# A graph attention kernel: layer 0's output transposed by the DMA crossbar, part of the D splits on GpSimd, two plain float32 v products in the prologue, and a new order of work

## Chip, cores, metric

One core of a Trainium2 chip. The metric is device time in microseconds, the median of some runs of the whole kernel; lower is better. In the profiles PE is TensorE, DVE is VectorE, ACT is ScalarE and POOL is GpSimd; SBUF is the memory on the chip that holds the tiles, and PSUM the one that TensorE writes its products to.

## The reference, cut to what matters

128 batch items x of 128 tokens by 512 features, a 128x128 adjacency `adj`. Layer 0 is a product with `adj`, a row maximum, a residual and a layer norm; layer 1 is attention with 8 heads under the mask `adj`, a projection, a layer norm and a residual, and one more norm.

```python
def L0(x, W1, W2, b):            # W1 = W2 = adj
    A = einsum('od,bdn->bon', W1, x);  C = einsum('od,bdn->bon', W2, x) + b[None, :, None]
    return max(relu(A[:, :, None, :] + (C - A)[:, :, :, None]), axis=-1)
def L1(x, w_qkv, w_proj, b_proj, gamma, beta, mask):
    q, k, v = split(x @ w_qkv)   # 8 heads
    a = softmax(where(mask == 0, -inf, q @ k.T * scale))
    o = (a @ v) @ w_proj + b_proj
    return o + layernorm(o) * gamma + beta
x = layernorm(x + L0(x, adj, adj, b))
x = layernorm(x + L1(x, w_qkv, w_proj, b_proj, gamma, beta, adj))
```

## The kernel before: the parts concerned

The kernel works in 32 groups of four items. Dense products are float32 made of float32r ones: each operand is split into a high part (a mask), a low part (a subtraction) and D, a combination of the two. HALF is 4096. Step (g, j) is a dense product of group g: 0 to 3 are v, 4 to 11 are q and k. "po" is the projection. `pm` and `pd` are the two PSUM tiles of one product, main and D; `pp` holds both in a double bank.

```python
def split(key, src, dsts):                       # VectorE: mask and low part
    _, fl, _ = dsts
    xh = work.tile([P, KC, P], FP, tag="xh")
    nc.vector.tensor_scalar(xh.bitcast(I32), src.bitcast(I32), HIGH, None, op0=ALU.bitwise_and)
    hs[key] = dsts, xh
    nc.vector.tensor_tensor(fl, src, xh, op=ALU.subtract)
def split_d(key):                                # VectorE, from its own mask xh
    (_, fl, fd), xh = hs[key]
    nc.vector.scalar_tensor_tensor(fd, fl.bitcast(FP), -HALF, xh, op0=ALU.mult, op1=ALU.add)
def split_high(key):                             # ScalarE
    (fh, _, _), xh = hs[key]
    nc.scalar.copy(fh, xh)
def transpose_x(b):                              # TensorE, into PSUM
    pts[b] = ps_1.tile([P, KC, P], FP, tag="ps1")
    for c in range(KC):
        nc.tensor.transpose(pts[b][:, c, :], xs[b][:, c * P : (c + 1) * P], ident)
def relu_0(b, n):                                # GpSimd, a few columns; then ScalarE adds it to x
    nc.gpsimd.tensor_scalar(r, r, b0_sb, 0.0, op0=ALU.add, op1=ALU.max)
def residual_x(b):                               # GpSimd, 128x512, all in SBUF
    nc.gpsimd.tensor_scalar(xbs[b], xbs[b], *c0s.pop(b), op0=ALU.mult, op1=ALU.add)
    nc.gpsimd.tensor_tensor(xbs[b], xbs[b], beta_sb, op=ALU.add)
# ... dense_main evicts pm (ScalarE), dense_rest adds pd (VectorE), conv, scores, softmax, norms cut
O = {...}     # positions of every part, in us of a planned TensorE time
plan.sort()   # the sorted plan fixes each engine's order; every engine runs its queue in that order
```

## Time and profile before

| what | value |
|---|---|
| time | 1993.17 us (1991.69 to 1994.87) |
| start of dense work, period of a steady group | 24.81 us, 60.47 us (32 groups) |
| one group of TensorE, DVE, ACT, POOL | 59.6, 51.3, 48.2, 30.7 us busy |

TensorE sets the period. The other engines have 9 us or more of slack a group on average; the kernel gives each of them one queue in a fixed order. The lines are in the prediction.

### The profile page before, as it was taken

What the parts mean: (1) busy time and instruction counts of PE and PEld (TensorE: products, weight loads), DVE (VectorE), ACT (ScalarE), POOL (GpSimd) and SP (SyncE); (2) the same over time, 40 slices, a digit from 0 to 9 for tenths busy, and PEclk for the clock granted to TensorE, in tenths of its full rate; (3) what the DMA queues carried; (4) which work ended last, traced back from release to release, by engine and by line L of the source; (5) the groups of instructions that cost most, each with busy time, mean ns of one, the idle gap of its engine ahead of it and who ended that gap; (6) DMA issues with size and microseconds to landing.
All of it is one profiled execution on the core that took longest, in us unless ns stands there. A gap on an engine that the chain in (4) does not pass through costs nothing. (4 is left out here: it accounts for less than half of the span.)

```text
span 1990.6 us, 33310 instructions
## 1 busy us (share of the span) xinstructions
PE 1921.3 (97%) x11041; PEld 1483.2 (75%) x11041; DVE 1676.0 (84%) x2615; ACT 1557.1 (78%) x4130; POOL 984.9 (49%) x1744
## 2 busy tenths in 40 slices
PE   6999999999999999999999999999999999999995
PEld 4777777777777777777777777777777777777774
DVE  7798888888888988888988888888889888888887
ACT  5887877778887778877778877788777788777875
POOL 2164455554555544554545555545555445545456
PEclk8999999999999999999999999999999999999998
DMA  4334444444443444454444444444434444444341
GB/s 121 108 107 128 127 117 126 119 127 128 116 128 106 117 133 127 112 135 120 117 128 121 123 123 117 130 129 113 132 106 117 133 128 112 136 119 117 107 112 58
DMA packets 337340, 237.90 MB, mean 120 GB/s; under 512 B 266512, under 2 KB 270736, under 8 KB 337168
## 3 DMA queue, kind: packets, MB, share of 16 engines
q1 hardware_dynamic: 336880, 235.72, 42.8%
q8 instruction: 87, 1.43, 0.3%
q14 instruction: 85, 0.70, 0.1%
q10 hardware_dynamic: 288, 0.07, 0.0%
HBM read 72.16 MB, written 98.57 MB: 86 GB/s over the span
## 5 line engine op out<-in xcount | busy, mean ns | idle before, releaser
L339 ACT ACTIVATE e<-e,nmax 128x128 f32<-128x128 f32 x1024 | 395.8, 389 | 21.6 <-DVE nmax L332 21.6
L437 ACT ACTIVATE square<-o,sum 128x512 bf16<-128x512 f32 x256 | 184.4, 720 | 145.2 <-DVE o L431 144.0
L354 ACT COPY planes<-e 128x2048 uint16<-128x2048 uint16 x124 | 234.3, 1889 | 60.8 <-DVE e L348 55.3
L443 POOL TENSOR_SCALAR sum<-sum 128x1 f32<-128x1 f32 (+1 forms) x322 | 82.5, 256 | 375.2 <-ACT square L437 369.2
L426 POOL TENSOR_TENSOR xb<-xb,o 128x512 f32<-128x512 f32 x124 | 203.9, 1645 | 85.3 <-DVE o L431 85.3
L444 POOL TENSOR_TENSOR sum<-sum,mhalf 128x1 f32<-128x1 f32 (+1 forms) x322 | 224.8, 698 | 26.8
L449 POOL TENSOR_SCALAR sum<-sum 128x1 f32<-128x1 f32 x256 | 82.4, 322 | 272.5 <-DVE o L431 271.2
L339 ACT ACTIVATION_READ_ACCUMULATOR e<-e,nmax 128x1 f32 x1024 | 192.6, 188 | 0.0
L409 POOL TENSOR_TENSOR xb<-xb,beta_sb 128x512 f32<-128x512 f32 x128 | 165.3, 1292 | 10.7
L348 DVE TENSOR_TENSOR e<-e,sums 128x1024 f32<-128x1024 f32 x128 | 166.8, 1303 | 4.4
L324 DVE SCALAR_TENSOR_TENSOR e<-psc,mask 128x1024 f32<-128x1024 f32 x128 | 153.3, 1218 | 18.4 <-PE psc L312 18.4
L464 ACT ACTIVATE o<-o,sum 128x512 f32<-128x512 f32 x128 | 103.7, 810 | 71.9 <-POOL sum L452 71.9
L332 DVE TENSOR_REDUCE nmax<-e 128x8 f32<-128x1024 f32 x128 | 155.0, 1211 | 0.0
L312 PEld LDWEIGHTS psc<-qkT 64*128 64x128 f32 x2048 | 124.3, 187 | 34.6 <-issue 23.5
L312 PE MATMUL psc<-qkT 64*128 64x128 f32 x2048 | 148.4, 285 | 0.0
L385 PE MATMUL pav<-eT,v 128*64 128x128 f32 x2048 | 133.0, 277 | 0.3 <-ACT eT L376 0.2
L179 PE MATMUL pa<-xt,adjT 128*128 128x512 f32 x256 | 126.9, 600 | 0.6 <-DVE adjT L104 0.4
L408 POOL TENSOR_SCALAR xb<-xb,sum 128x512 f32<-128x512 f32 x128 | 110.8, 866 | 23.4 <-DMA xb<-in_x_dram 22.9
L385 PEld LDWEIGHTS pav<-eT,v 128*64 128x64 f32 x2048 | 109.8, 137 | 13.7 <-issue 5.2
L456 DVE SCALAR_TENSOR_TENSOR o<-o,sum,gamma_sb 128x512 f32<-128x512 f32 x128 | 108.0, 844 | 1.0 <-POOL sum L449 0.8
L431 DVE SCALAR_TENSOR_TENSOR o<-o,sum,xb 128x512 f32<-128x512 f32 x128 | 99.0, 773 | 11.0 <-POOL sum L444 1.4
L225 PE MATMUL ptx<-ident,xt 128*128 128x128 f32 x512 | 85.2, 290 | 23.5 <-ACT xt L218 11.3
(4782 smaller groups left out, 5536.8 us busy)
## 6 DMA issues: line engine op xcount, KB each, us to landing
rows<-planes SPq DMA_DIRECT2D x124, 512.0 KB, 3.0
xt<-in_x_dram SPq DMA_DIRECT2D x128, 256.0 KB, 3.1
xb<-in_x_dram SPq DMA_DIRECT2D x128, 256.0 KB, 2.9
out_dram<-o SPq DMA_DIRECT2D x128, 256.0 KB, 2.1
wraw<-in_L_gnn_w_qkv_dram SPq DMA_DIRECT2D x12, 256.0 KB, 3.0
eT<-rows SPq DMA_TRANSPOSE x124, 4.9
wraw<-in_L_gnn_w_proj_dram SPq DMA_DIRECT2D x4, 256.0 KB, 4.4
gamma_sb<-in_L_gnn_ln_gamma_dram SPq DMA_DIRECT2D x1, 256.0 KB, 5.2
```

What stands on the lines that cost most here:

```text
L179: nc.tensor.matmul(pa[b], adjT, xs[b], start=True, stop=True)
L312: nc.tensor.matmul(psc[:, s, hp, :], qkT[hs, hp, i, :], qkT[hs, KC + hp, i, :], start=True, stop=True,)
L324: nc.vector.scalar_tensor_tensor(e, pscs.pop(b).rearrange("p s a m -> p (s a) m"), scale, mask_b, op0=ALU.mult, op1=ALU.add,)
L332: nc.vector.tensor_reduce(nmax, es[b], AX.X, ALU.max, negate=True)
L339: nc.scalar.activation(e[:, j, :], e[:, j, :], AF.Exp, bias=nmax[:, j : j + 1], accum_out=sums[:, j : j + 1],)
L348: nc.vector.tensor_tensor(e, e, sums[:, :, None].to_broadcast([P, H, P]), op=ALU.mult)
L354: nc.scalar.copy(planes, e.rearrange("p h m -> p (h m)").bitcast(U16).rearrange("p (m s) -> p s m", s=2),)
L385: nc.tensor.matmul(pavs[b][s * HD : (s + 1) * HD, hp, :], v[:, h * HD : (h + 1) * HD], eT[:, s * HP + hp, :], start=True, stop=True,)
L409: nc.gpsimd.tensor_tensor(xbs[b], xbs[b], beta_sb, op=ALU.add)
L426: engine.tensor_tensor(xbs[b], xbs[b], os[b], op=ALU.add)
L437: nc.scalar.activation(square, x, AF.Square, bias=s[:, 0:1], scale=-float(D), accum_out=s[:, 1:2],)
L444: nc.gpsimd.tensor_tensor(s, s, mhalf[:, :n], op=ALU.pow)
```

## The change

Intent: take layer 0's transposes off TensorE (a copy of x into two 16-bit planes, a store to DRAM and a crossbar read back); give GpSimd half of the D and one high copy; in the prologue run two v in plain float32 while the weights are split. To make D a plain subtraction, which GpSimd is then given, the splits are rescaled. The table of positions O is new as a whole.

```diff
+    def x_halves(b):
+        planes = work.tile([P, 2, D], U16, tag="xplanes", bufs=1)
+        nc.scalar.copy(planes, xs.pop(b).bitcast(U16).rearrange("p (m s) -> p s m", s=2))
+        nc.sync.dma_start(rows["x", b], planes)
+    def crossbar_x(b):
+        pts[b] = xpool.tile([P, KC, P], FP, tag="xt")
+        nc.sync.dma_start_transpose(pts[b]..., rows.pop(("x", b))...)
-    def split_d(key):
-        (_, fl, fd), xh = hs[key]
-        nc.vector.scalar_tensor_tensor(fd, fl.bitcast(FP), -HALF, xh, op0=ALU.mult, op1=ALU.add)
+    def split_high(key, gpsimd=False):
+        if gpsimd: nc.gpsimd.tensor_scalar(fh, xh, 1.0 / HALF, None, op0=ALU.mult)
+        else:      nc.scalar.activation(fh, xh, AF.Copy, scale=1.0 / HALF)
+    def split_d(key, gpsimd=False):
+        (fh, fl, fd), _ = hs.pop(key)
+        engine = nc.gpsimd if gpsimd else nc.vector
+        engine.tensor_tensor(fd, fh.bitcast(FP), fl.bitcast(FP), op=ALU.subtract)
+    def product_v(b):   # prologue: items 0 and 1 in plain float32
+        for kc in range(KC):
+            nc.tensor.matmul(pv, xraws[b][:, kc, :], raws[kc], start=(kc == 0), stop=(kc == KC - 1))
+ 'two': {'d': [0, 1, 1, 0, 0, 1, 0, 1], 'h': [1, 0, 0, 0, 0, 0, 0, 0], ...},   # 1: on GpSimd
   ... (copies and evictions of these, the planner, about 60 lines of positions: cut)
```

## The prediction, made before any run of the change

> **What bounds the kernel now.** I read the page's totals first, then a table of stretches, then the PE timeline of one group of four batch items, then the wait list, and last the other engines' timelines for that group.
>
> The totals and the stretch tables of the kernel before (columns: stretch, its length, busy time of PE, PEld, DVE, ACT, POOL with instruction counts, granted clock, DMA share, GB/s):
> ```profile
> span 1990.6 us, 33310 instructions
> PE 1921.3 (97%) x11041; PEld 1483.2 (75%) x11041; DVE 1676.0 (84%) x2615; ACT 1557.1 (78%) x4130; POOL 984.9 (49%) x1744
> ...
> 0.00:40.00 40.00, 25.05 (x77) 15.83 (x78) 27.96 (x48) 22.45 (x44) 11.49 (x35) 0.83 0.39 117
> 1060.50:1121.00 60.50, 59.56 (x346) 46.09 (x345) 51.27 (x81) 48.16 (x129) 30.72 (x55) 1.00 0.43 123
> 1945.00:1991.00 46.00, 25.75 (x156) 19.65 (x154) 32.00 (x54) 21.04 (x40) 27.64 (x51) 0.82 0.15 52
> ```
> In a steady stretch of one group PE has work in 59.56 of 60.5 us, at full clock. DVE has 51.3, ACT 48.2, POOL 30.7, and the DMA engines 0.43 of the time. So TensorE sets the period. In the timeline the score products of one group start at 1007.60 and of the next at 1068.07: a period of 60.47 us. There are 32 groups; the two ends (first 40 us, last 46 us) are the only places where PE idles much.
>
> What layer 0's transposes on TensorE cost, from the PE timeline (start, duration; a listed duration overlaps the next instruction, so I count from start to start) and, last line, the same transposes in the stretch table:
> ```profile
> 1023.13 1.16 PE L312 MATMUL psc<-qkT 64*128 64x128 f32 x16
> 1024.23 0.66 PE L225 MATMUL ptx<-ident,xt 128*128 128x128 f32 x4
> 1024.81 1.09 PE L385 MATMUL pav<-eT,v 128*64 128x128 f32 x16
> 1025.84 1.16 PE L312 MATMUL psc<-qkT 64*128 64x128 f32 x16
> 1026.93 1.09 PE L385 MATMUL pav<-eT,v 128*64 128x128 f32 x16
> 1027.95 0.66 PE L225 MATMUL ptx<-ident,xt 128*128 128x128 f32 x4
> 1028.37 0.48 PE L262 MATMUL pp_(16, 2)_10376<-w_h,x_h 128*128 128x512 f32 x1
> ...
> 1035.29 0.66 PE L225 MATMUL ptx<-ident,xt 128*128 128x128 f32 x4 [0.35 <-ACT v L297]
> ...
> 1060.50:1121.00 60.50, 2.63 (x16) 1.68 (x16) 5.49 (x8) 1.00 0.43 123
> ```
> The first sits in 1024.23 to 1024.81, 0.58 us. The next takes 1027.95 to 1028.37, 0.42. The last two stand between a product that starts at 1031.26 and one that starts at 1035.70: 4.44 us where a product without them takes 2.80 (1014.64 to 1017.44), so 1.64, with the 0.35 wait for a PSUM bank in it. Sum **2.64 us per group**.
>
> From the PE wait list:
> ```profile
> PE ptx L225 <- ACT v L297: 10.4, 30, 0.3
> PE pd_(22, 7)_13662 L270 <- ACT qkT L297: 0.5, 1, 0.5
> ```
> The first is that bank wait. The second is one of some thirty like it: the d product of dense step 7 waits 0.5 us in each group for a bank that ACT is still reading.
>
> **What the Trainium skill says.** "VectorE: DVE Perf Modes", section "The perf-mode tier table": a float32 tensor_scalar runs at twice the rate from SBUF, not from PSUM; a tensor_tensor in float32 stays at 1x. The trace agrees: the mask of 128x512 takes 682 ns from PSUM (x) and 420 ns from SBUF (weights); the subtraction takes 691 and 693. "GPSIMD Engine Reference", section "Elementwise — side-by-side cycle accounting": a float32 tensor_tensor is 1.96x slower on GpSimd. The trace has 1292 ns (beta add) against 693, 1.86x. "SBUF — State Buffer", section "SBUF: two separate sides": a GpSimd instruction and a DVE instruction with two SBUF inputs hold one port pair in turn, for the whole instruction. The trace agrees: the gamma multiplication is 0.74 us mostly, and 1.16 us at 1049.14, beside a GpSimd addition. "TensorE: Matmul & The Clock Gate", section "What's actually happening": half clock until some 3.4 us of sustained work. The trace has products at 0.43 us spacing at 25 us and 0.23 from 29.3 us on.
>
> **The change, part by part.**
>
> 1. Transposes off TensorE, for the 31 groups after the first: 31 x 2.64 = **82 us off the path**, if PE has its operands otherwise. Where the bank wait of step 7 comes from: a ring of four single banks is used by step 5 (two), one layer-0 product and step 7 (two), which makes five, so step 7 waits for step 5's eviction. The new order puts both layer-0 products after step 5 and then step 6, in the double-bank ring; step 8 comes 2.8 us later, and ptx no longer asks for a bank. I count 10 of the 30 x 0.5 = 15 us as **gained, 10 us**.
>
> 2. What comes for it, per group. ACT: four de-interleaving copies of 128x1024 16-bit values. The 2048-value copy of the softmax weights is 1.79 us start to start, and 512 values take some 0.5; on that line 1024 values take 0.93 us, so 3.7. One of the eight high copies goes to GpSimd: -0.5. So ACT has 48.2 + 3.2 = 51.4. DVE: four x masks now from SBUF, 4 x 0.26 = -1.0; four of eight D splits to GpSimd, 4 x 0.6 = -2.4: 47.8. GpSimd: four subtractions at 1.3 to 1.65 us (beta add alone, residual add with contention) and one scaling at about 0.87: +6 to +7.5, so about 37.5. DMA: the softmax path moves 128x2048 values through a store (512 KB, some 1.5 us of all engines) and a crossbar read (some 3.3 us at share 0.8 in the stretch 1049.5 to 1053.5); half of that for each x is 2.4 us, four times 9.6: 0.43 x 60.5 = 26 becomes some 36 us. Against a period of 57.5 that is ACT 89%, DVE 83%, GpSimd 65%, DMA 62%. None is the bound on average, so all of this lies beside PE. Latency of the new leg: copy 0.9, store 3.0, crossbar about 4 us; the layer-0 products run most of a group ahead of first use, so it fits.
>
> 3. Prologue. Dense work now starts at 24.81 us with a cold clock: its first product takes 4.53 us (24.81 to 29.34), 1.7 more than 2.80. Before it PE idles in gaps of 1.86, 3.91, 2.56, 1.15 and 1.43 us, because ACT normalizes one item at a time (ptx starts at 11.7, 16.3, 20.0, 22.3). The change interleaves the four chains, gives one normalization to DVE, and puts two float32 v of four layer-0-like products each into the gaps: 4 x 0.83 = 3.3 us warm, 5.4 cold. With transposes at about 11 and 13, v of item 0 until 18.5, x2, v of item 1 until 23.5, the last transpose, and mask and high of 1.3 us, dense begins at about 26, warm. That equals now (24.8 + 1.7 = 26.5); two split products fewer are 2 x 2.80 = 5.6 us. I take **5 us**.
>
> 4. The rescaling of the splits and d as h minus l cost ACT and DVE the same as before (631 for 610 ns, 691 for 686). d now waits for the high part too, a longer chain, not more PE work. The tail keeps its transposes on PE and changes order only: 0, plus or minus 3.
>
> Sum: 1993 - 82 - 10 - 5 = 1896. For new waits in a group that has less PE time to hide things I add 0.2 us per group, 6 us: **1902 us**, or 4.6% less.
>
> **The rivals.**
> - *ACT takes the bound.* For it: 51.4 of 57.5 us leaves 6 us, and it is in-order with evictions PE needs soon. Against: its gaps now (12 us per group) are named as waits for DVE and POOL results, not as lack of time. If a third of the gain goes to late evictions: about 1930.
> - *The D splits on GpSimd come late.* A GpSimd D takes twice as long, and POOL's order mixes it with statistics that wait for ACT (369 us of waits at L443) and DVE. Two of the four belong to projections, whose d product starts only 1.87 us after the first. For: the plan puts them close before that. Against: POOL idles half of the time. If two D products per group come 0.5 us late: 31 us, about 1933.
> - *The crossbar becomes late or crowded.* Eight transposes per group go through one in-order queue that also loads x and xb. For: during a softmax transpose the DMA share is already near 1. Against: the share on average stays near 0.6 and a leg of 8 us has tens of us of room. If it blocked once per group for 1 us: about 1930.
> - *The whole step-7 wait and the stated sum come true, no new wait*: about 1889.
>
> **Range and chances.** The sum lies near the best case; the rivals are each worth some 30 us and I give each under 10%; that two strike together is unlikely. Hence **1902 us**, eight in ten between **1886 and 1930**. The 2% line is at 1953; to miss it the gain would have to be less than 40 of about 95 us. Faster **0.95**, same 0.045, slower 0.005.
>
> **What would show it.** Right: no transposes ptx after the first group; a steady period of 57.2 to 58.0 us with PE busy over 98% of it; ACT at about 51, DVE at 48, POOL at 37 to 38 us per group; a DMA share near 0.6; no step-7 bank wait; first dense product near 26 us at full clock, and the second group's start some 5 us earlier. Wrong: a period above 58.5 us, with PE waiting for x_d, od (GpSimd), for x_l after the crossbar, or for evictions by ACT; or a prologue that starts dense work after 29 us.

## The result

The changed kernel takes **2086.48 us** (2083.74 to 2087.69, 4 runs), the kernel before 1993.81 in the same rounds: ratio 1.0464, 95% interval 1.0446 to 1.0482. A ratio is the mean time of one kernel's fast runs over that of the other's of the same rounds, so not quite the ratio of the medians. Below, a run's time is compared with the kernel before on its own chip (1993 to 1995 us).

The page's totals after:

```profile
span 2085.8 us, 33259 instructions
PE 1902.1 (91%) x10537; PEld 1422.0 (68%) x10537; DVE 1690.5 (81%) x2486; ACT 1646.7 (79%) x4221; POOL 1268.9 (61%) x1906
```

TensorE shows 504 instructions fewer, about as meant, but is busy 91% of a longer span in place of 97%. The stretch from 300 to 1800 us in the table of stretches (length, busy time of PE, PEld, DVE, ACT, POOL, clock, DMA share, GB/s), before and then after:

```profile
300.00:1800.00 1500.00, 1476.79 (x8525) 1142.68 (x8524) 1270.54 (x1985) 1192.82 (x3162) 761.15 (x1345) 1.00 0.44 123
```

```profile
300.00:1800.00 1500.00, 1400.87 (x7845) 1049.30 (x7844) 1236.68 (x1816) 1217.87 (x3125) 944.99 (x1408) 1.00 0.58 151
```

TensorE lost 99 us of these 1500, at full clock. Start to start of step 4, the period of most groups went from 60.47 to about 62.57 us (means of groups 4 to 28: 60.5 and 62.8). The 95.2 us that the span grew by are: dense work starts at 28.00 and not at 24.81 (+3.2); groups 0 and 1 take 131.8 and not 110.8 us (+21.0); groups 2 to 31 take +69.8; the tail +1.1.

Where TensorE waits in the steady part: its timeline after, one group (start, duration, instruction, and in brackets the idle time and who ended it):

```profile
1030.94 1.20 PE L317 MATMUL pp_('o', 58)_9894<-p_d,od 128*128 128x512 f32 x4 [0.94 <-DVE od L275]
...
1034.09 0.50 PE L309 MATMUL pm_('o', 59)_9947<-p_h,oh 128*128 128x512 f32 x1 [0.24 <-ACT oh L270]
...
1038.35 0.47 PE L309 MATMUL pp_(16, 4)_9991<-x_h,w_h 128*128 128x512 f32 x1 [0.77 <-DVE o L478]
...
1057.97 1.20 PE L317 MATMUL pd_(16, 11)_10129<-x_d,w_d 128*128 128x512 f32 x4 [1.45 <-ACT qkT L344]
```

The old waits (0.35 for ptx, 0.5 at step 7) are gone. Summed over all steady groups from 300 to 1800 us, TensorE's waits went from 21.7 to 96.8 us: the D product of step 11 for ScalarE's eviction 34.4 (24 times), po2 for VectorE's `od` 25.4, step 4 for a bank that VectorE's eviction frees 18.6, and smaller ones: 6.4 for transfers of the softmax weights, 2.6 for a D of GpSimd.

**Two of these waits come from turns at the SBUF port.** Two of VectorE's instructions in the kernel before, undisturbed:

```profile
1028.97 0.68 DVE L239 SCALAR_TENSOR_TENSOR od<-ol,xh_('o', 62)_10355 128x512 fp32r<-128x512 f32 x1
...
1033.15 0.75 DVE L431 SCALAR_TENSOR_TENSOR o<-o,sum,xb 128x512 f32<-128x512 f32 x1
```

The same two, and some behind them, in the changed kernel before the first wait (columns as above):

```profile
1027.60 1.59 DVE L478 SCALAR_TENSOR_TENSOR o<-o,sum,xb 128x512 f32<-128x512 f32 x1
...
1029.12 1.76 DVE L275 TENSOR_TENSOR od<-oh,ol 128x512 fp32r<-128x512 f32 x1
...
1033.26 0.68 DVE L348 TENSOR_TENSOR v<-v,pd_(15, 3)_9873 128x512 f32<-128x512 f32 x1
1033.86 1.31 DVE L261 TENSOR_SCALAR xh<-xT 128x512 int32<-128x512 int32 x1
```

and GpSimd's:

```profile
1027.19 1.45 POOL L473 TENSOR_TENSOR xb<-xb,o 128x512 f32<-128x512 f32 x1
1028.61 1.72 POOL L275 TENSOR_TENSOR x_d<-x_h,x_l 128x512 fp32r<-128x512 f32 x1
1030.31 0.65 POOL L496 TENSOR_SCALAR sum<-sum 128x1 f32<-128x1 f32 x1
...
1033.60 1.29 POOL L275 TENSOR_TENSOR x_d<-x_h,x_l 128x512 fp32r<-128x512 f32 x1 [1.45 <-ACT x_h L270]
```

Read the two together. VectorE's `o` at 1027.60 (0.75 us undisturbed) begins beside GpSimd's `xb` and ends 0.55 us after it. GpSimd's D at 1028.61 (1.29 undisturbed) waits in turn for `o` and ends at 1030.33. VectorE's `od` at 1029.12 (0.69 undisturbed) ends at 1030.88, 0.55 after that, and TensorE's product begins at 1030.94. Then even GpSimd's one-column operation (0.22) takes 0.65. The mask at 1033.86 (0.42) takes 1.31. The addition at 1033.26, with one input in PSUM, keeps its 0.68, though GpSimd's D starts at 1033.60 beside it. The second wait, 1038.35, is the end of the same queue of stretched VectorE work. Per group VectorE's time over its undisturbed durations is 5.2 us; it was 1.0 in the kernel before. How much of this is due to GpSimd's D, the runs below show; GpSimd's residual and statistics take turns too.

**The third comes from ScalarE's queue.** GpSimd, then ScalarE, ahead of the wait at 1057.97:

```profile
1045.94 2.12 POOL L455 TENSOR_SCALAR xb<-xb,sum 128x512 f32<-128x512 f32 x1 [1.11 <-DMA xb<-in_x_dram]
1048.15 1.61 POOL L456 TENSOR_TENSOR xb<-xb,beta_sb 128x512 f32<-128x512 f32 x1
...
1055.58 0.30 POOL L196 TENSOR_SCALAR rm<-rm,b_sb 128x2 f32<-128x2 f32 x1
```

```profile
1055.91 0.72 ACT L202 ACTIVATE xt<-xt,rm 128x512 f32<-128x512 f32 x1 [1.98 <-POOL rm L196]
...
1057.34 0.57 ACT L344 ACTIVATE qkT<-pm_(16, 7)_10111 128x512 f32<-128x512 f32 x1
```

A relu of two columns stands in GpSimd's queue behind a residual whose load came late. ScalarE waits 1.98 us for it, and the eviction that frees TensorE's bank stands behind that addition.

### The profile page after: what moved, and what is told of

Same layout as the page of the kernel before. It is cut to its first block, busy times and chain, and to the rows that moved or that the text cites.

```text
span 2085.8 us, 33259 instructions
## 1 busy us (share of the span) xinstructions
PE 1902.1 (91%) x10537; PEld 1422.0 (68%) x10537; DVE 1690.5 (81%) x2486; ACT 1646.7 (79%) x4221; POOL 1268.9 (61%) x1906
## 4 chain that ended last, share of the span: by engine, by line
PE 30%; DVE 29%; POOL 15%; ACT 9%; DMA 8%; issue 8%; DVEq 0%; SPq 0%; ACTq 0%; POOLq 0%
DVE o L478 5%; POOL sum L491 4%; DMA xb<-in_x_dram 4%; DMA eT<-rows 3%; PE pav L432 3%; DVE xh L261 3%; POOL xb L455 3%; ACT xt L202 3%; PE psc L359 3%; DVE o L464 3%; DVE od L275 2%; DVE x_d L275 2%; POOL xb L456 2%; DVE nmax L379 2%; DVE x_l L263 2%
## 5 line engine op out<-in xcount | busy, mean ns | idle before, releaser
L401 ACT COPY planes<-e 128x2048 uint16<-128x2048 uint16 x124 | 234.5, 1891 | 23.1 <-DVE e L395 23.1
L491 POOL TENSOR_TENSOR sum<-sum,mhalf 128x1 f32<-128x1 f32 (+1 forms) x322 | 216.7, 673 | 26.8
L490 POOL TENSOR_SCALAR sum<-sum 128x1 f32<-128x1 f32 (+1 forms) x322 | 99.8, 310 | 170.2 <-ACT square L484 151.2
L456 POOL TENSOR_TENSOR xb<-xb,beta_sb 128x512 f32<-128x512 f32 x128 | 193.6, 1512 | 10.7
L455 POOL TENSOR_SCALAR xb<-xb,sum 128x512 f32<-128x512 f32 x128 | 156.9, 1226 | 50.5 <-DMA xb<-in_x_dram 45.7
L473 POOL TENSOR_TENSOR xb<-xb,o 128x512 f32<-128x512 f32 x124 | 175.8, 1418 | 5.1 <-DVE o L478 0.3
L275 POOL TENSOR_TENSOR od<-oh,ol 128x512 fp32r<-128x512 f32 x60 | 83.2, 1386 | 126.8 <-ACT oh L270 122.7
L478 DVE SCALAR_TENSOR_TENSOR o<-o,sum,xb 128x512 f32<-128x512 f32 x128 | 128.6, 1005 | 25.8 <-POOL sum L491 17.7
L202 ACT ACTIVATE xt<-xt,rm 128x512 f32<-128x512 f32 x128 | 91.3, 713 | 62.1 <-POOL rm L196 57.1
L275 POOL TENSOR_TENSOR x_d<-x_h,x_l 128x512 fp32r<-128x512 f32 x65 | 96.8, 1491 | 60.4 <-ACT x_h L270 31.8
L244 ACT COPY xplanes<-xt 128x1024 uint16<-128x1024 uint16 x124 | 129.0, 1040 | 5.0 <-DMA rowsx<-xplanes 4.1
```

The lines of the kernel that those rows point to most:

```text
L275: engine.tensor_tensor(fd, fh.bitcast(FP), fl.bitcast(FP), op=ALU.subtract)
L401: nc.scalar.copy(planes, e.rearrange("p h m -> p (h m)").bitcast(U16).rearrange("p (m s) -> p s m", s=2),)
L473: engine.tensor_tensor(xbs[b], xbs[b], os[b], op=ALU.add)
L478: nc.vector.scalar_tensor_tensor(os[b], in0, scalar, in1, op0=ALU.mult, op1=ALU.add, accum_out=s[:, 0:1],)
L491: nc.gpsimd.tensor_tensor(s, s, mhalf[:, :n], op=ALU.pow)
```

## The experiments

18 kernels ran; the first six of the text (`e1`, `e2`, `e4`, `e6`, `e9`, `e10`) have two timed runs each, the others four. "Excess" is VectorE's time per group over its undisturbed durations, about the shortest of the same instruction (from its timeline, ten groups; another choice of these durations moves a value by up to 0.4 us). "Period" is the mean over groups 4 to 28. The remaining runs are in the text.

| kernel | us | ratio to before | period |
|---|---|---|---|
| before | 1993.8 | 1 | 60.5 |
| changed | 2086.5 | 1.0464 | 62.8 |
| changed, no D on GpSimd | 2215.8 | 1.1116 | 66.7 |
| changed, x transposed on TensorE | 2182.2 | 1.0947 | 66.3 |
| changed, no plain v | 2093.5 | 1.0502 | 63.0 |
| changed, relu on VectorE | 2055.8 | 1.0308 | 61.8 |
| changed, fills for GpSimd's D | 2031.5 | 1.0188 | 61.2 |
| changed, both of these | 1986.2 | 0.9956 | 59.6 |
| before, rescaled splits | 2073.9 | 1.0401 | 63.2 |
| before, rescaled, D from the mask | 1995.7 | 1.0007 | 60.6 |
| changed, reordered | 1936.8 | 0.9722 | 58.5 |
| before, reordered | 1934.8 | 0.9707 | 58.7 |
| changed, reordered, fills for GpSimd's D | 1913.0 | 0.9586 | 57.8 |

In the expectations, single letters stand for theories. P: the turns at the port are to blame. X: the crossbar. O: the order of the queues. Q: only GpSimd's lateness. S: D's new wait for ScalarE's copy. H: the late relu.

### Taking one part of the change back

**No D and no high copy on GpSimd** (`e1_no_pool`):

```diff
- 'd': [0, 1, 1, 0, 0, 1, 0, 1], 'first_d': [1, 1, 0, 1], 'first_h': [1, 1, 0, 0], 'h': [1, 0, ...]
+ 'd': [0] * 8, 'first_d': [0] * 4, 'first_h': [0] * 4, 'h': [0] * 8
```

> The changed kernel with all D splits on DVE and all high copies on ACT again (nothing of the splits on GpSimd); crossbar, float32 v and the whole order kept. Theory P (GpSimd and DVE take turns at the SBUF ports, which stretches DVE by 5.3 us per group against 1.0 before, and in a stretch of 34 us without any DVE idle this makes the od of po2 and the banks of dense 4 late): the stretch of DVE falls to about 1.5 us per group, the waits of PE for od at po2 (1.06 us per group) and for the bank at dense 4 (0.78) shrink, period from 62.6 to about 60.5 to 61.5 us, time about 2030 to 2060. Rival O (the fixed order, tuned to other durations, is the cause, whichever engine does the D): DVE gets 4 x 0.6 us more to do, period 62.5 or more, time 2085 or more.

Measured 2215.84: P's number missed by far, and what O expected (2085 or more) came. VectorE's excess fell only to about 3.6, not to 1.5. The new waits, in TensorE's timeline:

```profile
1039.60 1.20 PE L317 MATMUL pd_('o', 55)_9327<-p_d,od 128*128 128x512 f32 x4 [3.16 <-DVE od L275]
```

TensorE waits 119.6 us from 300 to 1800 us for the D of po1 and po3, which GpSimd makes in the changed kernel; here they stand in VectorE's queue behind work of other steps. So this run does not test the turns alone, and it does not speak for P: it shows how closely the order and the places of the parts hang together.

**x transposed on TensorE again** (`e2_x_on_pe`, the four transposes back in the plan, `transpose_x` in place of `crossbar_x`).

> The changed kernel with the transposes of x on TensorE again in every group (at the places of the order of before), no de-interleaving copy, no store, no crossbar read for x; D splits on GpSimd, float32 v and the rest kept. Rival X (the crossbar leg, its copies on ACT and its transfers, makes the waits): ACT gets 3.7 us per group back, the waits fall by some 3 us while the transposes come back with 2.3 to 2.7 us: period 61 to 62, time about 2060. Theory P: the waits for DVE and GpSimd stay and the transposes are added, and the x mask reads PSUM again, not contended: period 63.5 to 65, time 2110 to 2150.

Measured 2182.19, more than either theory expected: without the crossbar this order is 96 us worse. Like the run before, it puts work back into an order that was not made for it, and TensorE's waits (94.7 us) now have other names, so it clears the crossbar only in part. What speaks against X besides: of the changed kernel's 96.8 us only 6.4 are waits for a transfer, and the run with both edits below keeps the crossbar and has 34.8 us of waits left.

**No plain v** (`e4_no_v`: the two `('v', k)` out of the prologue's order).

> The changed kernel without the two float32 v in the prologue: v 0 and 1 of the first group are made as split products like all others. The steady period does not change (62.6). My prediction's view: dense work starts some 3 us earlier but two split products of 2.8 us are back: within 3 us of 2086. Rival V (the float32 v hold raw weights and banks, and delay the start by the 25 us that the first three groups lose): time about 2065.

Measured 2093.48 (two runs, 2090.67 and 2096.29), 7 us more than the changed kernel, but the intervals of the two ratios overlap (1.0459 to 1.0546, 1.0446 to 1.0482). In the profile the prologue gains nothing from the v. This run's first split product:

```profile
28.38 0.77 PE L309 MATMUL pp_(0, 4)_253<-x_h,w_h 128*128 128x512 f32 x1 [3.90 <-ACT x_h L270]
```

Dense work starts 0.4 us later than with the v (28.00), but group 2 starts at 157.2 us, against 159.8 in the changed kernel and 156.8 to 160.5 in three other runs with the v and the same order. So a gain from the v isn't shown; that they delay the start by some 20 us (V) is refuted.

### Putting one part into the kernel before

**Rescaled splits with half of D and one high copy on GpSimd** (`e6_before_pool`):

```diff
+ 'two': {'d': [0, 1, 1, 0, 0, 1, 0, 1], 'h': [1, 0, 0, 0, 0, 0, 0, 0], ...}   # and split_high, split_d of the change
```

> The kernel before (transposes on TensorE, old order) with one part of the change alone: splits rescaled, d as h minus l, and the same half of the D splits and one high copy per group on GpSimd. Theory P: DVE's stretch per group rises from 1.0 to 3 to 4 us, GpSimd's ops are longer, PE waits for D or for late evictions: period from 60.5 to 61.5 to 63, time 2025 to 2080. Rival O: DVE is relieved by 2.4 us per group and nothing is late in an order that had room: within 1% of 1993.

Measured 2104.98, 111 us more than before and more than either theory expected; VectorE's excess rose to about 3.3, as P said.

**GpSimd work of another kind at the same eight places**, reading SBUF (`e9_hold_read`, and `e11_hold_read_1` with one addition a place) or only writing it (`e10_hold_write`, three fills a place):

```diff
+    def hold():
+        for _ in range(3):     # e11: 1;  e10: 3 of memset(scratch, 0.0)
+            nc.gpsimd.tensor_tensor(scratch, gamma_sb[:, :192], beta_sb[:, :192], op=ALU.add)
+            at(min(u + O["x_d"][i], first + 1.8), hold)    # and the same after each od
```

> The kernel before with nothing changed but eight extra pieces of GpSimd work per group, one after each D split in the plan: three additions of 128x192 that read two constant tiles in SBUF and write a scratch tile nobody reads. No data dependence on anything. Theory P (a GpSimd instruction that reads SBUF and a DVE instruction with two SBUF inputs take turns): DVE's stretch per group rises from 1.0 us to 3 or more, D splits and gamma products become longer, period rises by 0.5 us or more. Rival Q (only GpSimd's own queue matters: what it does late is late): the same rise as in the run with writes alone.

> The same as the run with reads, but the extra GpSimd instructions are fills of the same 128x192 scratch tile, which read nothing. Theory P: DVE instructions with two SBUF inputs keep their length, DVE's stretch stays within 0.5 us per group of before, period within 0.2 us of 60.47 unless GpSimd's lateness matters. Rival Q: as slow as the run with reads, per microsecond of GpSimd time added.

> The kernel before, with one GpSimd addition of 128x192 float32 (both inputs in SBUF) at each of the eight places per group where the D are computed: about 0.77 us each by the run with three at each place, so some 6.2 us a group, the same GpSimd time as the run with fills, which changed nothing (1993.05). P (turns at the SBUF port: what costs is GpSimd work that reads SBUF while VectorE reads two operands from SBUF): VectorE's excess over its undisturbed times rises by some 0.6 us a group and GpSimd's own by more, 2000 to 2060 us. Q (only the lateness of GpSimd's queue costs, whatever it does): as with the fills, 1991 to 1998 us.

Measured 2225.02, 1993.05 and 2002.94. The three additions add 18.5 us of GpSimd work a group, the three fills 6.2, so the first pair mixes reading with amount; VectorE's excess rose only to 2.0 us, and ScalarE waited 231.1 us for GpSimd's statistics (71.9 before). The fair pair is the fills against one addition: 6.2 us of fills a group cost nothing that shows (two runs, interval -0.51 to +0.49%), and 5.4 us of reading cost 0.44% (interval 0.26 to 0.61). These intervals overlap, so the times alone don't tell the two apart. The traces do: VectorE's excess stays as it was with the fills and rises by 0.3 us with the additions. In the old order the turns are a small thing.

**The control: rescaled splits, all on VectorE and ScalarE** (`e7_before_scale`, as `e6` with every 'd' and 'h' 0), and the same with D from the mask (`e17_before_scale_mask`):

```diff
-        engine.tensor_tensor(fd, fh.bitcast(FP), fl.bitcast(FP), op=ALU.subtract)
+        nc.vector.scalar_tensor_tensor(fd, xh, 1.0 / HALF, fl.bitcast(FP), op0=ALU.mult, op1=ALU.subtract)
```

> The kernel before with the changed kernel's rescaled splits (high copy scaled by ScalarE, D = h - l as a plain subtraction that waits for that copy), but all of it on VectorE and ScalarE: the control for the run that also put half of D and one high copy on GpSimd (2104.98). P and Q (GpSimd is to blame there): 1993 to 2035 us, so GpSimd accounts for 70 us or more of the 111. S (the new dependence of D on ScalarE's high copy is to blame): 2070 us or more.

> The control of the last batch (before with the rescaled splits, all on VectorE and ScalarE, 2073.93) with one edit: D is computed as xh/HALF - l from the mask's result, which VectorE itself made, in place of h - l from the scaled copy of ScalarE. Same instruction count, same values, same place in the order. S (the new wait of VectorE's D for ScalarE's copy, in two in-order queues, is what cost the 80 us): 1993 to 2010 us. If the rescaling cost it in another way (the weights' extra scaled copies, the forms): above 2050 us.

Measured 2073.93 and 1995.65. No engine has more to do in the first, yet it costs 80 us; one changed input takes all of it away. How a copy that VectorE waits for does this, in the timelines of the first run (ScalarE, VectorE, TensorE):

```profile
1016.75 0.82 ACT L469 ACTIVATE o<-o,sum 128x512 f32<-128x512 f32 x1 [1.23 <-POOL sum L457]
1017.47 0.61 ACT L246 ACTIVATE x_h<-xh 128x512 fp32r<-128x512 f32 x1
```

```profile
1018.12 1.64 DVE L251 TENSOR_TENSOR x_d<-x_h,x_l 128x512 fp32r<-128x512 f32 x1 [1.73 <-ACT x_h L246]
1019.68 0.68 DVE L237 TENSOR_SCALAR xh<-ptx 128x512 int32<-128x512 int32 x1
1020.39 0.69 DVE L239 TENSOR_TENSOR x_l<-ptx,xh 128x512 fp32r<-128x512 f32 x1
```

```profile
1021.19 1.10 PE L183 MATMUL pa<-xt,adjT 128*128 128x512 f32 x2 [2.00 <-issue]
```

ScalarE waits for a statistic of GpSimd, the copy `x_h` waits behind it, VectorE's D waits 1.73 us for the copy, and the mask and subtraction that empty a PSUM tile wait behind D. `pa`, TensorE's next product, starts 0.11 us after that subtraction's end; that it waits for that tile is my reading, the profile only says "issue". Over the whole run VectorE's D waits 63.9 us (63 times) for `x_h`; in the run with D from the mask this wait is gone. Of the 111 us of the run with D on GpSimd, S explains 80; the other 31 came with GpSimd's share.

### The same edits in the changed kernel

**D of VectorE from the mask** (`e15_d_from_mask`, the edit above where `gpsimd` is false), **relu on VectorE** (`e3_relu_dve`), **both** (`e16_mask_relu`):

```diff
-        nc.gpsimd.tensor_scalar(r, r, b0_sb, 0.0, op0=ALU.add, op1=ALU.max)
+        nc.vector.tensor_scalar(r, r, b0_sb, 0.0, op0=ALU.add, op1=ALU.max)
```

> The changed kernel with one edit: the relu on the four-column maxima of layer 0 goes from GpSimd to VectorE (a 128x2 operation). H (the wait of step 11 comes from GpSimd's late relu, which holds ScalarE's addition and by its order the qkT eviction): the wait of 1.4 us before pd of step 11 goes and the period falls by about 1 us, 2040 to 2060 us. P alone (the turns take up VectorE's time, and another wait ends last as soon as this one goes): within 10 us of 2086, with the wait moved to another step.

> The changed kernel with the same edit to the D that stay on VectorE; the D on GpSimd still read ScalarE's copy. S: the wait of po2 for VectorE's od (25.4 us over the 24 groups from 300 to 1800 us, 1.06 us a group) goes, and with it about 31 x 1.0 = 30 us: 2050 to 2065 us. P (od is late because VectorE was held at the port): the wait stays, within 10 us of 2086.

> Both edits: D on VectorE from the mask's result, and layer 0's relu on VectorE (alone 2055.76, with po2's wait for od left at 22.2 us over 24 groups). S and H together: both waits go, another 0.9 us a group: 2020 to 2035 us, period near 60.3 us, with the bank wait of step 4 (18.6 us over 24 groups) left as the largest. P: within 10 us of 2056.

Measured 2055.76, 2090.86 and 2060.66. H holds: TensorE's waits at step 11 went from 34.4 us to none and the time fell by 31 us. S, worth 80 us in the old order, is worth nothing here: po2 still waited 30.7 us for `od` in the second run. The dependence was there but did not end last; the turns did.

**Fills in place of GpSimd's D** (`e19_fill_d`; wrong arithmetic, the D products get zeros; D is a small correction):

```diff
+        if gpsimd:
+            nc.gpsimd.memset(fd.bitcast(FP), 0.0)
+            nc.gpsimd.memset(fd.bitcast(FP), 0.0)
+            fh, fl, fd = (t[:, 0, :4] for t in (fh, fl, fd))    # a small subtraction keeps the waits
```

> The changed kernel, wrong on purpose: each D on GpSimd is replaced by two fills of the same tile (a fill of 128x192 took 0.258 us, so an estimate of 2 x 0.69 = 1.4 us for 128x512, near the 1.49 us of the D) and a subtraction of 128x4, so that GpSimd's time, its waits and the order stay, and only its reading of SBUF goes. P (turns at the port): VectorE's excess (5.3 us a group) falls by 2 us or more, the wait for po2's od goes, 2000 to 2060 us. O (the order and the queues): within 15 us of 2086.

Measured 2031.54, 55 us less than the changed kernel. Groups of instructions (busy us, mean ns | idle before), changed kernel and then this run:

```profile
L263 DVE TENSOR_TENSOR x_l<-xT,xh 128x512 fp32r<-128x512 f32 x124 | 115.4, 931 | 9.5 <-PE pm_(0, 2)_586 L310 4.4 <-PE pm_(0, 9)_511 L310 0.8
...
L275 DVE TENSOR_TENSOR od<-oh,ol 128x512 fp32r<-128x512 f32 x60 | 73.5, 1225 | 48.5 <-ACT oh L270 48.5
```

```profile
L263 DVE TENSOR_TENSOR x_l<-xT,xh 128x512 fp32r<-128x512 f32 x124 | 86.1, 695 | 7.0 <-PE pm_(0, 2)_592 L314 1.9 <-PE pm_(0, 9)_517 L314 0.8
...
L279 DVE TENSOR_TENSOR od<-oh,ol 128x512 fp32r<-128x512 f32 x60 | 41.2, 686 | 48.8 <-ACT oh L270 48.8
```

VectorE's `od` went from 1225 to 686 ns and `x_l` from 931 to 695 without an edit of theirs. Excess 5.2 to 3.2 us; po2's wait for `od` 25.4 to 7.5 us; the bank wait of step 4 is gone; step 11's stayed (34.9). P holds, for two of the three waits. It is not all of the excess: about half of the rise from 1.0 stays with the fills. A pair of fills and the small subtraction take 1.3 us (526 and 553 ns a fill, about 0.25 the subtraction), a D 1.39 to 1.49 with its own turns, so GpSimd has nearly the same to do.

One thing changed besides the reading. The fills need no input, so they can run while GpSimd waits for ScalarE's copy:

```profile
1003.32 0.53 POOL L276 MEMSET x_d<- 128x512 f32 x1
1004.31 0.38 POOL L279 TENSOR_TENSOR x_d<-x_h,x_l 128x4 fp32r<-128x4 f32 x1 [0.46 <-ACT x_h L270]
```

GpSimd's idle time for ScalarE fell from 15.4 to 10.3 us a group, so its D came sooner. That alone doesn't explain the gain: TensorE had waited only 2.6 us of 1500 for a D of GpSimd, and VectorE's idle time for GpSimd stayed at 1.0 us a group while its busy time fell by 2.2. How much the earlier D helped in other ways was not tried in this order.

**Both: fills and relu** (`e20_fill_d_relu`).

> The changed kernel with both edits: fills in place of GpSimd's D (alone 2031.54, 55 us less) and the relu on VectorE (alone 2055.76, 31 us less). If the causes are separate they add: 2086.5 - 55 - 31 = about 2000, within 8 us, with the wait of step 11 (34.9 us over 24 groups in the run with fills) gone. If they share one wait: 2015 to 2031. What is left above 1993 would then be the first two groups (21 us) and nothing would be left of the 82 us that the transposes were to give.

Measured 1986.22: 100 us less than the changed kernel, more than 55 + 31, and 14 us below what was expected of separate causes (about 2000, within 8). Removing both is enough to undo the whole loss of 93 us. The first two groups still take 127.4 us (110.8 in the kernel before), and the steady period is 0.9 us better than before.

### The same parts in another order

A search off the chip over the position tables proposed new orders; it only proposed, and what follows rests on the chip. **Changed kernel reordered** (`e12_reordered`), **without D on GpSimd** (`e13_reordered_no_pool`), **kernel before reordered** (`e14_before_reordered`):

```diff
- 'conv_max': ...    # about 60 lines of positions, all replaced
- 'd': [0, 1, 1, 0, 0, 1, 0, 1], 'h': [1, 0, 0, 0, 0, 0, 0, 0]
+ 'd': [0, 0, 1, 0, 0, 1, 0, 1], 'h': [0, 0, 0, 0, 0, 1, 0, 0]    # e12; e13: all 0; e14 has none
```

> The changed kernel's parts in another order: only the table of positions is changed (and which three of the eight D and which one high copy per group are GpSimd's: a D fewer than in the changed kernel, 3 in place of 4). O (the order is what cost): 1900 to 1960 us, below before, with the waits of steps 4, 11, po2 mostly gone. P (the parts themselves cost too much VectorE time at the port, whatever the order): 2040 us or more.

> The crossbar and the v trick alone, no D and no high copy on GpSimd, in an order of its own: VectorE has 2.1 us a group more of its own work and fewer turns. If GpSimd's D are worth having once the order suits them: 10 to 40 us above the reordered run with them (1920 to 1990). If the turns eat what they save: equal or faster than that run.

> The control: the kernel before's parts, treated with the same search for an order. If the old order was already close to the best, 1985 to 2000 us; the estimate from the durations of the trace is that some 40 us may be left (1940 to 1960). Whatever the reordered changed kernel gains beyond this run is the worth of the change's parts; if it gains nothing beyond it, the parts are worth nothing and only the order counts.

Measured 1936.80, 1960.33 and 1934.81. The same kinds of work in another order take 150 us less than the changed kernel (with three D on GpSimd in place of four); dense work starts at 26.2 us, groups 0 and 1 take 112.4, so the loss of the first groups was the order's too. The kernel before gains as much from an order of its own: the stretch of the reordered kernel before, then of the reordered changed one:

```profile
300.00:1800.00 1500.00, 1499.92 (x8735) 1180.04 (x8734) 1322.24 (x2047) 1218.45 (x3262) 829.55 (x1381) 1.00 0.47 126
```

```profile
300.00:1800.00 1500.00, 1473.46 (x8350) 1137.53 (x8349) 1269.74 (x1976) 1306.31 (x3357) 958.17 (x1493) 1.00 0.62 162
```

In the first, TensorE has no wait at all. With both orders searched in the same way the change is worth nothing: 0.9722 against 0.9707, with intervals that overlap. How good each search's order is isn't known. With the crossbar, the order found with D on GpSimd beats the one found without (1936.8 against 1960.3); these two differ in their positions as well, so the 24 us aren't D's alone.

**Reordered, with fills** (`e22_reordered_fill`, the fill edit in the reordered changed kernel; it computes wrong D too).

> The reordered changed kernel (1936.80) with fills in place of GpSimd's D: the same test in the new order. If that order has already taken the D out of the way of VectorE's SBUF-only instructions (its excess is 2.1 us a group against 5.3): within 6 us of 1937. If the turns still hold it back: 1925 us or less.

Measured 1913.00, 24 us less: the turns still cost that much in the new order, where the excess is 2.1 us and falls to 1.2. Here GpSimd's idle time for ScalarE did not fall (15.9 and 16.2 us a group), so an earlier D is an unlikely rival here. TensorE's wait that goes is the bank wait of step 4 (14.7 us of 26.0 between 300 and 1800; the others are mostly DMA's):

```profile
1015.02 0.47 PE L309 MATMUL pp_(17, 4)_10598<-x_h,w_h 128*128 128x512 f32 x1 [0.64 <-DVE o L478]
```

The fastest versions that compute what they should are the two reordered ones, 2.8 and 2.9% below before.

## Why the prediction was wrong

- **Right:** the transposes left TensorE, the waits for ptx and at step 7 went, ACT has 50.8 us a group (predicted 51.4; 1217.87 x 62.57 / 1500), the DMA share is 0.58 (about 0.6). GpSimd has 39.4 us (37.5; its one scaling took 2.0 and not 0.87). Of the prediction's signs of being wrong, a period above 58.5 with waits for `od` and for ScalarE's evictions came; a wait after the crossbar did not. A slower kernel had been given a chance of 0.005.
- **Step 2 failed:** "None is the bound on average, so all of this lies beside PE." Averages were nearly right and did not matter. The prediction had quoted the turn-taking and its trace, then allowed for it in GpSimd's time (1.3 to 1.65 us a D) and not in VectorE's. Shown: VectorE has 51.6 us a group, not 47.8 (the terms sum to 47.9), and its excess is 5.2, not 1.0; fills in place of D give back 55 us. The masks that moved from PSUM to SBUF, counted as -1.0 us, became instructions that take turns (0.42 or 1.31 us; their mean is 0.65 where the prediction had 0.42).
- **The allowance for new waits failed:** 0.2 us a group was taken, TensorE's waits grew by 3.2 us ((96.8 / 23.97) - (21.7 / 24.8), the groups in 1500 us). The rivals had under 10% each. Late evictions on ScalarE did strike (34.4 us), but not because ScalarE was full: GpSimd's relu held them, as the run with the relu on VectorE shows (31 us). D late on GpSimd hardly struck (2.6 us). What came late was VectorE's own work, its `od` (25.4) and its eviction for step 4 (18.6), and no rival had that. "Two strike together is unlikely" took the causes as separate; VectorE, GpSimd and ScalarE wait for each other, so one late engine makes the others late.
- **Step 1 was too large:** 2.64 us a group, 82 in all. Without waits TensorE needs 58.7 us with the transposes (reordered before) and some 57.2 without (57.76 less waits of 13.5 us in 26 groups): 1.5 us, an estimate of 47 us in all. The trace of the reordered kernel before agrees: its transposes take 1.56 us a group, start to start and without a wait. The 2.64 held the 0.35 us wait for a bank and gaps that a better order removes with the transposes still there. (The rival's best case, by its own terms, is 1891 and not 1889.)
- **Step 3 was wrong in sign:** not -5 but +24 us to the start of group 2. It had the start at about 26 and warm; dense work starts at 28.00 and its first product takes 4.33 us (28.00 to 32.33), no better than the 4.53 before. The two v take 4.6 and 3.6 us of TensorE, as counted, and the last transpose starts at 23.83, as foreseen. But its mask starts at 26.51, behind a D that took 1.58 us and a split of weights in VectorE's queue, where the prediction had 1.3 us for mask and high copy together; and a gain from the v isn't shown. Later in the first group ScalarE's queue holds normalizations, a plane copy and copies of weights ahead of an eviction; TensorE's timeline after:

```profile
28.00 0.76 PE L309 MATMUL pp_(0, 4)_269<-x_h,w_h 128*128 128x512 f32 x1 [3.54 <-ACT x_h L270]
...
59.65 2.08 PE L317 MATMUL pd_(0, 11)_460<-x_d,w_d 128*128 128x512 f32 x4 [5.63 <-ACT qkT L344]
```

  The reordered kernel keeps the v, starts at 26.18 with a first product of 2.90 us, and loses only 3 us of these 24, so it is the order; which of its positions, was not tried.
- **Step 4** ("a longer chain, not more PE work", cost 0) is wrong in the old order by 80 us and right in the changed one, where another wait ends last. In a tuned order the price of a dependence belongs to the order.
- **Open:** which positions of the new orders matter; whether D on GpSimd can be had without the 24 us; what the two v are worth; what stretches the other half of VectorE's excess in the changed order; whether the buffer that the change took from the o tiles (four to three) costs anything.

## What to carry to other kernels

Where several in-order engines feed one that is nearly always busy, slack on average says little: before moving work to an idle engine, list which instructions it will run beside, whether both use SBUF only, and what stands behind each in its queue. Judge a change of parts only after giving the old parts an order of the same quality: here a new order alone was worth 3% to the old kernel, and the parts nothing beyond it in the orders that were found. And test a suspected dependence in the kernel where it is suspected: the same edit was worth 80 us in one order and none in the other.

## What the Trainium skill lacked or had wrong

- "SBUF — State Buffer", section "SBUF: two separate sides", is right on the turns, and these runs agree: VectorE with two SBUF inputs, and a 2x mask from SBUF, wait for GpSimd (0.69 to 1.76 us, 0.42 to 1.31), and with one PSUM input they don't (0.68). It lacks what this means for a choice: moving an operand from PSUM to SBUF makes an instruction faster alone and exposed to GpSimd.
- The same section: a fill on GpSimd reads nothing, and 6.2 us of it a group cost nothing that shows, while 5.4 us of reading cost 9 us in one order, and fills in place of four D gave back 55 us in another. The page has the rule, no case of such a size.
- "GPSIMD Engine Reference", section "3.1 Elementwise — side-by-side cycle accounting", has 1.96x for tensor_tensor for 2048 elements; undisturbed D of 512 elements here: 1.29 us against 0.69, 1.87x. It has no number for a single-input scaling into float32r: 1.50 to 2.00 us for 128x512, where the two-step scaling of the residual in float32 takes 0.77. The cause was not tried.
- No page that I read tells how to cost a wait between two in-order queues; the runs show one copy's dependence at 80 us and a two-column relu at 31 us.
